# One set of products with ones for a step's two key tiles, after VectorE has added their numerators

## The chip, the cores and the metric

The kernel runs on one core of a Trainium2 chip. A core has a matrix engine (TensorE, in the profile PE, with its weight loads as PEld), three engines for elementwise work (VectorE as DVE, ScalarE as ACT, GpSimd as POOL) and queues that start DMA transfers (SP among them). The engines run side by side, each works through its own instructions in order, and they wait for each other through semaphores. Matrix products land in PSUM, which has eight banks of 512 fp32 columns.

The metric is device time of one execution in microseconds (us), lower is better.

## The reference

One transformer block on `x` of shape (2, 1024, 128), all in fp32: attention, then a mixture of experts. Cut to what matters:

```python
q = (x @ wq).reshape(Bq, Tq, N_KV, N_REP, HEAD_DIM)      # 2 groups of 4 heads
k_lat = (x @ wk_down).reshape(Bq, Tq, N_KV, D_LAT)       # 32 wide
v_lat = (x @ wv_down).reshape(Bq, Tq, N_KV, D_LAT)
k = jnp.einsum('bkhl,ld->bkhd', k_lat, wk_up)
v = jnp.einsum('bkhl,ld->bkhd', v_lat, wv_up)
scores = jnp.einsum('bqhrd,bkhd->bhrqk', q, k) * scale
scores = jnp.where(causal, scores, jnp.finfo(scores.dtype).min)
probs = jax.nn.softmax(scores, axis=-1)
y = jnp.einsum('bhrqk,bkhd->bqhrd', probs, v)
...
x = x + _layernorm(attn(_layernorm(x)))
x = x + _layernorm(moe(_layernorm(x)))    # 32 experts, top 6 of 2 of 4 groups; 16 anchors; shared
```

The softmax divides each query's weighted sum of values by the sum of its numerators over all keys. That sum of numerators is what the change is about.

## The kernel before, in words

**Folding.** The up-projections are folded into the queries and into the output weights, so that keys and values are used 32 wide. Four heads of a group then share TensorE: their 32-row or 32-column strips work side by side.

**Units and steps.** Attention runs over units `(b, g, q)`: batch, group of four heads, block of 256 queries (`QC`). Batch 0 goes through its blocks upwards, batch 1 downwards. A unit has `q + 1` steps `s`, and each step has two key tiles of 128 keys (`pieces`, line 450). A step with `s < q` is full: both tiles count for all 256 queries. The step `s == q` lies on the diagonal: the second tile counts only for the upper 128 queries. There are 40 steps in 16 units, 24 full and 16 on the diagonal.

**What a step does.**
- `numerators` (456): TensorE writes the scores of four heads, keys by queries, into four PSUM banks (464) and adds minus the query's maximum (478). ScalarE takes the exponential into an SBUF tile `pr` (484), 128 keys x 4 heads x up to 512 columns: the first tile's queries, then the second's. On the diagonal GpSimd sets what the mask hides to zero (487). `pr` has three buffers.
- `values` (497): TensorE multiplies `pr` with the values and accumulates in the left half of the bank `o` (501), 32 partitions for a head.
- `sums` (507): TensorE multiplies the same `pr` with a matrix of ones and accumulates in the right half of `o` (510). Each of the 32 rows of a head then holds the sum over the keys.
- After a unit's last step ScalarE copies `o` to SBUF (517) and `normalized` (520) divides: two ScalarE operations, then three of VectorE (530 to 532), put off by `tick`.

**The maxima ahead.** The maxima of later units are found in items (`maxima`, 388): products of queries with keys into four banks `sm` (399), the mask (409), and four or eight reductions on VectorE (416). After a unit's last item, `split` (427) cuts the maxima into three bf16 parts on VectorE, `turn` (436) transposes them on TensorE (443), and VectorE copies the result to `mT` (447), which line 478 reads.

**Order.** The order on TensorE, VectorE, ScalarE and GpSimd is that of the program text. For each step the loop at 575 writes: the scores and numerators of this step, the values of the step before (`weigh`), a transposition if one is ready, a `tick`, one item of maxima, the sums of the step before, another `tick`, and sometimes one more item. A `tick` advances side work by a piece: the normalization, the projections of later tokens (`project`), and from the end of batch 0 on its output projection and routing (`route`, 609: many small VectorE operations, lines 674 to 748).

**PSUM.** Seven banks are handed out in turn under one tag, for the scores, the maxima, the transpositions and all side work. The eighth is `o`.

After attention come the experts (762): 20 chunks for each of four blocks of 512 tokens, three products of 512 columns each, with routing rows that SP loads.

Of the kernel before, what the change touches and what calls it, by code (L numbers as in the profile page):

```python
# [10 lines left out]
F32 = mybir.dt.float32  # L11
BF16 = mybir.dt.bfloat16
AF = mybir.ActivationFunctionType
ALU = mybir.AluOpType
# [3 lines left out]
P = 128  # L18
# [7 lines left out]
def attn_moe_block(  # L26
# [34 lines left out]
    nc = tc.nc  # L61
    B, T, D = x.shape
    NT = T // P
    QC = 256
# [6 lines left out]
    L = wk_up.shape[0]  # L71
    G = wk_down.shape[1] // L
    R = NH // G
    scale = float(P) ** -0.5
    E, _, MI = w_gate.shape
    A, _, AI = anchor_w_gate.shape
# [10 lines left out]
    work = ctx.enter_context(tc.tile_pool(name="work", bufs=2))  # L87
# [3 lines left out]
    def bank(name, dtype=F32):  # L91

        return psum.tile([P, 2048 // mybir.dt.size(dtype)], dtype, tag="s", name=name, bufs=7)

    def acc(name):
        return psum.tile([P, 512], F32, tag="o", name=name, bufs=1)
# [83 lines left out]
    ones32 = const.tile([P, L], F32, name="ones32")  # L180
# [11 lines left out]
    def tables(name):  # L192

        if name != loaded[0]:
            nc.scalar.preload_act_table_set(name)
            loaded[0] = name
# [6 lines left out]
    def tick():  # L203
        for queue in (ends, side):
            while queue:
                if next(queue[0], queue) is not queue:
                    break
                queue.pop(0)
# [30 lines left out]
    def awake(n):  # L239

        idle = bank("idle")
        for _ in range(n):
            nc.tensor.matmul(
                idle, lhsT=ones, rhs=ones.unsqueeze(1).to_broadcast([P, 4, P]),
                start=True, stop=True,
            )
# [189 lines left out]
    def turn(u):  # L436

        b, g, q = u
        parts = neg_parts[units.index(u) % len(neg_parts)]
        pt = bank(f"pm{b}{g}{q}", BF16)  # L440

        for i, j in enumerate((*range(TQ), TQ - 1)):
            nc.tensor.transpose(
                pt[:, ts(i, P)], parts[:, j, :, :].rearrange("p r l -> p (r l)"), ident_bf
            )
        mT = work.tile([P, QC + P], BF16, tag="mT", name=f"mT{b}{g}{q}", bufs=6)
        nc.vector.tensor_copy(mT, pt[:, 0 : QC + P])  # L447
        negT[u] = mT

    def pieces(u, s):  # L450

        if s < u[2]:
            return [(2 * s, 0, 0, QC), (2 * s + 1, QC, 0, QC)]
        return [(2 * s, 0, 0, QC), (2 * s + 1, QC, P, P)]

    def numerators(u, s):

        b, g, q = u
        qT, kT, _ = qkv[b]
        banks = [bank(f"s{b}{g}{q}{s}") for _ in range(R)]  # L460
        for i, (kt, at, lo, n) in enumerate(pieces(u, s)):
            for r in range(R):
                rows = ts(r, L)
                nc.tensor.matmul(  # L464
                    banks[r][:, at : at + n], lhsT=kT[rows, g, ts(kt, P)],
                    rhs=qT[rows, g, q * QC + lo : q * QC + lo + n], start=(i == 0), stop=False,
                    skip_group_check=True,
                )
        mT = negT[u]
        m = at + n  # L470
        for r in range(R):
            rows = ts(r, L)
            if s < q:
                less = mT[rows, 0:QC].unsqueeze(1).to_broadcast([L, 2, QC])
                dst = banks[r].rearrange("p (i c) -> p i c", c=QC)
            else:
                less, dst = mT[rows, :], banks[r][:, 0:m]
            nc.tensor.matmul(  # L478
                dst, lhsT=ones[rows, :], rhs=less, start=False, stop=True, skip_group_check=True
            )  # L480
        tables(EXP_LN)
        pr = work.tile([P, R, 2 * QC], F32, tag="wide", name=f"pr{b}{g}{q}{s}", bufs=3)
        for r in range(R):
            nc.scalar.activation(pr[:, r, 0:m], banks[r][:, 0:m], AF.Exp)  # L484
        if s == q:
            own = pr.rearrange("p r (i c) -> p r i c", c=QC)[:, :, :, 0:P]
            nc.gpsimd.affine_select(  # L487
                out=own, in_=own, compare_op=ALU.is_ge, fill=0.0, base=0,
                pattern=[[0, R], [0, 2], [1, P]], channel_multiplier=-1,
            )  # L490
        return pr
# [5 lines left out]
    def values(u, s, pr, o):  # L497
        b, g, _ = u
        for kt, at, lo, n in pieces(u, s):
            for r in range(R):  # L500
                nc.tensor.matmul(  # L501
                    o[ts(r, L), lo : lo + n], lhsT=qkv[b][2][:, kt, ts(g, L)],
                    rhs=pr[:, r, at : at + n],
                    start=(kt == 0), stop=False, skip_group_check=True,
                )

    def sums(u, s, pr, o):
        for kt, at, lo, n in pieces(u, s):
            for r in range(R):
                nc.tensor.matmul(  # L510
                    o[ts(r, L), QC + lo : QC + lo + n], lhsT=ones32,
                    rhs=pr[:, r, at : at + n], start=False, stop=True, skip_group_check=True,
                )
        b, g, q = u
        if s == q:
            t = work.tile([P, 2 * QC], F32, tag="raw", name=f"raw{b}{g}{q}", bufs=3)
            nc.scalar.copy(t, o)
            ends.append(normalized(u, t))

    def normalized(u, t):  # L520

        b, g, q = u
        own, total = t[:, 0:QC], t[:, QC : 2 * QC]
        r = work.tile([P, QC], F32, tag="rsum", name=f"rsum{b}{g}{q}", bufs=2)
        tables(EXP_LN)
        nc.scalar.activation(r, total, AF.Ln)
        nc.scalar.activation(r, r, AF.Exp, scale=-1.0)
        yield
        ot[u] = work.tile([P, QC], F32, tag="ot", name=f"ot{b}{g}{q}", bufs=NU + 2)
        nc.vector.scalar_tensor_tensor(total, total, -1.0, r, ALU.mult, ALU.mult)  # L530
        nc.vector.tensor_tensor(own, own, r, ALU.mult)
        nc.vector.scalar_tensor_tensor(ot[u], total, 2.0, own, ALU.add, ALU.mult)
        yield

    def attention(done_with):
        items = [(u, gen) for u in units for gen in [maxima(u)] for _ in range(u[2] + 1)]
        through = {u: i + 1 for i, (u, _) in enumerate(items)}


        need = [through[units[0]]]  # L540
        for k in range(1, len(steps)):
            ahead = steps[min(k if k < 4 else k + 1, len(steps) - 1)][0]
            need.append(max(need[-1], through[ahead]))
        done = 0
        turned = 0
        finished = 0

        def one_item():
            nonlocal done, finished
            u, gen = items[done]  # L550
            while projected.get((u[0], u[2] * QC // BC), -1) < u[1]:
                tick()
            assert units.index(u) < turned + len(neg_parts)
            next(gen)
            done += 1
            finished += through[u] == done

        def turn_ready(upto):
            nonlocal turned
            while turned < upto:  # L560
                turn(units[turned])
                turned += 1

        o = {}
        waiting = None

        def weigh(entry):
            u, s, pr = entry
            while projected.get((u[0], u[2] * QC // BC), -1) < G:
                tick()  # L570
            if s == 0:
                o[u] = acc(f"o{u[0]}{u[1]}{u[2]}")
            values(u, s, pr, o[u])

        for k, (u, s) in enumerate(steps):
            while done < need[k]:
                one_item()
                if k == 0:
                    tick()
                    awake(3)  # L580
            ready = finished
            turn_ready(units.index(u) + 1)
            pr = numerators(u, s)
            if waiting:
                weigh(waiting)
            turn_ready(ready)
            tick()


            if done < len(items):  # L590
                one_item()
            if waiting:
                last = waiting[0]
                sums(*waiting, o[last])
                if last[0] != u[0]:
                    done_with(last[0])
            waiting = (u, s, pr)
            tick()
            if any(need[j] - done > j - k - 1 for j in range(k + 1, len(steps))):
                one_item()  # L600
                tick()
        weigh(waiting)
        sums(*waiting, o[waiting[0]])
        done_with(waiting[0][0])


# [282 lines left out]
```

## Time and profile before

Three runs took 479.04, 480.38 and 480.4 us. The profiled execution is one more execution, and all durations below come from it.

| | us |
|---|---|
| median of the runs | 480.38 |
| span of the profiled execution | 478.7 |
| PE busy (share of the span) | 453.1 (95%) |
| DVE busy | 303.3 (63%) |
| ACT busy | 219.6 (46%) |
| POOL busy | 33.5 (7%) |
| products with values, line 501: 640 instructions, busy | 39.4 |
| products with ones, line 510: 640 instructions, busy | 39.3 |
| first score product to last product with ones (attention) | 19.2 to 233.3 |

How to read it: busy time is the time in which an engine had work in flight. It doesn't say who waits for whom; that is in the chain of waits (followed back from the last instruction, at each step to what released it) and in the order of time. An fp32 product is two instructions of TensorE, so that 320 products with ones are 640 instructions. In a row such as `128x512 f32<-128x512 f32 x80 | 58.0, 725 | 2.7` come the shape written and read, the count, the busy time, the mean of one in ns, and the idle time of the engine before them. `x16 ... 1.00` in the chain of waits is a piece of 16 instructions that took 1.00 us.

### The profile page before, as it was taken

The page shows a single profiled execution, that of the slowest core. Times are in us where ns is not written, and L with a number is a line of the kernel's source. Part 1 is how long each engine was busy: PE and PEld are TensorE (multiplying, and loading weights), DVE is VectorE, ACT ScalarE, POOL GpSimd, SP SyncE. Part 2 cuts the span into 40 slices and gives each one's busy share as a digit, 9 for nine tenths or more (in the row PEclk, how much of TensorE's full clock was granted, in tenths as well). Part 3 has the DMA queues.
Part 4 walks back from the last instruction along what each step waited for, and adds up shares of the span by engine and source line. Part 5 has one row for each costly group of instructions (what it writes and reads, how often), then busy time and mean ns, then how long its engine had stood idle before and what let it go on. Part 6 is the DMA issues. An engine that isn't in the chain of part 4 may idle for free.

```text
span 478.7 us, 8959 instructions
## 1 busy us (share of the span) xinstructions
PE 453.1 (95%) x3427; PEld 223.7 (47%) x3427; DVE 303.3 (63%) x943; ACT 219.6 (46%) x427; POOL 33.5 (7%) x55
## 2 busy tenths in 40 slices
PE   8997999999999999988869999999999999999991
PEld 5554554544555555555345444544434444344440
DVE  4468766466756887797335575489656755466552
ACT  3454556554554747746642646432225422252222
POOL 2000000000000201002100110000001100001001
PEclk9999999999999999999979999999999999999996
DMA  7820000000000000000521333223151353124100
GB/s 218 222 86 1 2 1 2 1 1 3 1 1 3 2 1 3 1 2 19 176 68 55 100 109 96 66 83 109 51 163 60 118 134 109 66 91 136 58 1 22
DMA packets 27355, 29.26 MB, mean 61 GB/s; under 512 B 8272, under 2 KB 16112, under 8 KB 27312
## 3 DMA queue, kind: packets, MB, share of 16 engines
q1 hardware_dynamic: 26976, 28.15, 19.5%
q8 instruction: 27, 0.44, 0.4%
q10 hardware_dynamic: 336, 0.54, 0.3%
q14 instruction: 16, 0.13, 0.1%
HBM read 27.23 MB, written 1.44 MB: 60 GB/s over the span
## 4 chain that ended last, share of the span: by engine, by line
PE 70%; DVE 16%; issue 10%; ACT 1%; DMA 1%; POOL 0%; POOLq 0%; ACTq 0%; DVEq 0%
PE pg L775 12%; PE pu L776 12%; PE oacc L785 11%; DVE nm L416 8%; PE sm L399 7%; PE s L464 5%; PE o L501 4%; PE o L510 4%; PE pp L352 3%; PE po L621 2%; DVE parts L432 2%; PE psh L791 2%; DVE nm L434 1%; PE s L478 1%; PE sm L409 1%
## 5 line engine op out<-in xcount | busy, mean ns | idle before, releaser
L416 DVE TENSOR_REDUCE nm<-sm 128x1 f32<-128x512 f32 (+2 forms) x192 | 92.7, 548 | 53.1 <-PE sm L409 37.0
L780 DVE TENSOR_TENSOR hid<-hid,pu 128x512 f32<-128x512 f32 x80 | 54.8, 686 | 75.9 <-PE pu L776 56.8
L484 ACT ACTIVATE pr<-s 128x512 f32<-128x512 f32 (+1 forms) x160 | 75.5, 558 | 55.5 <-PE s L478 55.5
L779 ACT ACTIVATE hid<-pg 128x512 f32<-128x512 f32 x80 | 47.8, 597 | 115.5 <-PE pg L775 103.5
L775 PE MATMUL pg<-hT,wg_sb 128*128 128x512 f32 x160 | 83.4, 603 | 0.0
L776 PE MATMUL pu<-hT,wu_sb 128*128 128x512 f32 x160 | 82.1, 594 | 0.0
L785 PE MATMUL oacc<-hid,wd_sb 128*128 128x512 f32 x160 | 80.9, 595 | 0.0
L781 DVE TENSOR_TENSOR hid<-hid,spread 128x512 f32<-128x512 f32 x80 | 58.0, 725 | 2.7
L776 PEld LDWEIGHTS pu<-hT,wu_sb 128*128 128x128 f32 x160 | 30.7, 192 | 38.8 <-issue 37.9
L785 PEld LDWEIGHTS oacc<-hid,wd_sb 128*128 128x128 f32 x160 | 30.1, 190 | 39.3 <-issue 31.5
L464 PE MATMUL s<-qT,kT 32*128 32x256 f32 (+1 forms) x640 | 46.9, 381 | 1.0 <-DVE nm L416 1.0
L775 PEld LDWEIGHTS pg<-hT,wg_sb 128*128 128x128 f32 x160 | 29.3, 192 | 35.7 <-issue 34.8
L399 PE MATMUL sm<-kT,qT 32*128 32x512 f32 (+3 forms) x384 | 44.3, 525 | 0.8 <-DVE nm L416 0.3
L501 PE MATMUL o<-pr,v 128*32 128x256 f32 (+1 forms) x640 | 39.4, 364 | 2.1 <-POOL pr L487 1.9
L464 PEld LDWEIGHTS s<-qT,kT 32*128 32x128 f32 x640 | 32.0, 184 | 16.2 <-issue 10.1
L510 PE MATMUL o<-pr,ones 128*32 128x256 f32 (+1 forms) x640 | 39.3, 363 | 0.0
L487 POOL TENSOR_SCALAR_AFFINE_SELECT pr<-pr 128x1024 f32<-128x1024 f32 x16 | 17.8, 1112 | 196.3 <-ACT pr L484 196.3
L501 PEld LDWEIGHTS o<-pr,v 128*32 128x32 f32 x640 | 16.7, 109 | 23.2 <-issue 10.1
L510 PEld LDWEIGHTS o<-pr,ones 128*32 128x32 f32 x640 | 17.0, 109 | 20.5 <-issue 11.6
L399 PEld LDWEIGHTS sm<-kT,qT 32*128 32x128 f32 x384 | 16.8, 183 | 11.9 <-issue 4.2
L826 POOL TENSOR_TENSOR y<-y,x 128x512 f32<-128x512 f32 x4 | 5.1, 1267 | 192.3 <-DVE y L295 150.7
L478 PE MATMUL s<-mT,ones 32*128 32x512 bf16 (+1 forms) x160 | 16.9, 353 | 1.5 <-DVE mT L447 1.5
(163 smaller groups left out, 365.1 us busy)
## 6 DMA issues: line engine op xcount, KB each, us to landing
spread<-cw_rows SPq DMA_DIRECT2D x128, 128.0 KB, 2.9
spread<-cw_rows SPq DMA_DIRECT2D x64, 64.0 KB, 2.0
out_dram<-y SPq DMA_DIRECT2D x4, 256.0 KB, 2.3
x<-in_L_attn_x_dram SPq DMA_DIRECT2D x2, 256.0 KB, 4.1
wq_sb<-in_L_attn_wq_dram ACTq DMA_DIRECT2D x2, 256.0 KB, 4.2
wo_sb<-in_L_attn_wo_dram SPq DMA_DIRECT2D x1, 512.0 KB, 6.5
x<-in_L_attn_x_dram SPq DMA_DIRECT2D x1, 512.0 KB, 7.6
cw_rows<-cwT SPq DMA_DIRECT2D x4, 96.0 KB, 1.9
```

The source lines that it names most:

```text
L399: nc.tensor.matmul(banks[r][:, at : at + k1 - k0], lhsT=qT[ts(r, L), g, ts(qt, P)], rhs=kT[ts(r, L), g, k0:k1], start=(at == 0), stop=Fals ...
L416: nc.vector.tensor_reduce(nm[:, k0 // BC, j, r : r + 1], banks[r][:, at : at + k1 - k0], AX.X, ALU.max, negate=True,)
L464: nc.tensor.matmul(banks[r][:, at : at + n], lhsT=kT[rows, g, ts(kt, P)], rhs=qT[rows, g, q * QC + lo : q * QC + lo + n], start=(i == 0), ...
L484: nc.scalar.activation(pr[:, r, 0:m], banks[r][:, 0:m], AF.Exp)
L501: nc.tensor.matmul(o[ts(r, L), lo : lo + n], lhsT=qkv[b][2][:, kt, ts(g, L)], rhs=pr[:, r, at : at + n], start=(kt == 0), stop=False, skip ...
L510: nc.tensor.matmul(o[ts(r, L), QC + lo : QC + lo + n], lhsT=ones32, rhs=pr[:, r, at : at + n], start=False, stop=True, skip_group_check=True,)
L775: nc.tensor.matmul(pg, lhsT=wg_sb[:, c, :], rhs=hT[:, cols], start=True, stop=True)
L776: nc.tensor.matmul(pu, lhsT=wu_sb[:, c, :], rhs=hT[:, cols], start=True, stop=True)
L779: nc.scalar.activation(hid, pg, AF.Silu)
L780: nc.vector.tensor_tensor(hid, hid, pu, ALU.mult)
L781: nc.vector.tensor_tensor(hid, hid, spread, ALU.mult)
L785: nc.tensor.matmul(oacc, lhsT=wd_sb[:, c, :], rhs=hid, start=False, stop=(c == NCH - 1))
```

## The change

`paired` adds, on VectorE, the numerators of a step's two key tiles for all four heads in one instruction, into an SBUF tile `pair` with a single buffer. `sums` multiplies this with ones in place of the two tiles. On a full step that is 1,024 columns added (4 heads x 256) and four products of 256 columns in place of eight. On the diagonal the second tile counts only for the upper 128 queries: these 128 columns a head are added (512 in all), four products of 128 columns take them, and four more take the lower 128 queries from `pr`, in place of four of 256 and four of 128. The addition for a step is written after the scores and numerators of the step that follows, ahead of its `weigh`; for the last step, ahead of the last `weigh`.

```diff
-    def sums(u, s, pr, o):
-        for kt, at, lo, n in pieces(u, s):
+    def paired(u, s, pr):
+
+        pair = work.tile([P, R, QC], F32, tag="pair", name=f"pair{u[0]}{u[1]}{u[2]}{s}", bufs=1)
+        (_, _, _, n0), (_, at, lo, n) = pieces(u, s)
+        nc.vector.tensor_tensor(
+            pair[:, :, lo:n0], pr[:, :, lo:n0], pr[:, :, at : at + n], ALU.add
+        )
+        return [pair[:, :, lo:n0], pr[:, :, 0:lo]] if lo else [pair]
+
+    def sums(u, s, pair, o):
+        hi = QC
+        for part in pair:
+            lo = hi - part.shape[2]
             for r in range(R):
                 nc.tensor.matmul(
-                    o[ts(r, L), QC + lo : QC + lo + n], lhsT=ones32,
-                    rhs=pr[:, r, at : at + n], start=False, stop=True, skip_group_check=True,
+                    o[ts(r, L), QC + lo : QC + hi], lhsT=ones32,
+                    rhs=part[:, r, :], start=False, stop=True, skip_group_check=True,
                 )
+            hi = lo
...
             pr = numerators(u, s)
+            pair = paired(*waiting) if waiting else None
             if waiting:
                 weigh(waiting)
...
-                sums(*waiting, o[last])
+                sums(*waiting[0:2], pair, o[last])
...
+        pair = paired(*waiting)
         weigh(waiting)
-        sums(*waiting, o[waiting[0]])
+        sums(*waiting[0:2], pair, o[waiting[0]])
         done_with(waiting[0][0])
```

## The prediction

> **What bounds the kernel now.** I read the page's head and its chain of waits, then the busy time stretch by stretch, then the order of time.
>
> ```profile
> span 478.7 us, 8959 instructions
> ...
> PE 70%; DVE 16%; issue 10%; ACT 1%; DMA 1%; POOL 0%; POOLq 0%; ACTq 0%; DVEq 0%
> ```
>
> PE's 70% of the chain makes it look like the only bound. The stretches, cut at the first score product of a step (start:end, length, then busy time of PE, PEld, DVE, ACT, POOL), say otherwise:
>
> ```profile
> 42.77:51.80 9.03, 7.79 (x95) 4.33 (x89) 8.69 (x24) 4.30 (x12) 1.10 (x1) 1.00 0.01 2
> ...
> 116.84:134.55 17.71, 17.58 (x255) 8.52 (x251) 11.93 (x27) 9.13 (x19) 1.10 (x1) 1.00 0.01 2
> ...
> 160.15:184.28 24.13, 22.92 (x346) 12.24 (x342) 20.85 (x70) 17.56 (x41) 4.01 (x5) 1.00 0.01 2
> 184.28:195.97 11.69, 11.69 (x159) 7.15 (x155) 5.64 (x15) 7.72 (x16) 1.42 (x5) 1.00 0.00 1
> 195.97:224.92 28.95, 26.03 (x394) 14.85 (x390) 27.36 (x164) 16.76 (x35) 3.51 (x3) 1.00 0.01 2
> ```
>
> At 116.84 (one unit of four steps) PE is full and VectorE has 5.8 us free. At 42.77, 160.15 and 195.97 VectorE is 96%, 86% and 95% busy: there the reductions of the maxima and, from 160, the routing of batch 0 fill it. The order of time in the free stretch shows how near the two engines stand:
>
> ```profile
> 118.92 1.14 PE L399 MATMUL sm<-kT,qT 32*128 32x512 f32 x8
> ...
> 120.00 0.86 PE L510 MATMUL o<-pr,ones 128*32 128x256 f32 x16
> 120.08 2.48 DVE L416 TENSOR_REDUCE nm<-sm 128x1 f32<-128x512 f32 x4 [1.67 <-PE sm L399]
> 120.78 1.17 PE L464 MATMUL s<-qT,kT 32*128 32x256 f32 x16
> ```
>
> Four reductions start 0.09 us after their products end and take 2.48. The next step's scores (L464) take four of seven PSUM banks in turn, and the fourth is the bank of the first reduction. That one took about 0.68 (L416, 128x512), so its bank is free some 0.75 after 120.08, at 120.83, while PE is there at 120.78. Line 416's own view names the wait:
>
> ```profile
> who waited for it (us, times):
>   PEld s L464: 2.3, 4
> ```
>
> So products with ones that become shorter bring L464 forward only until the first reduction is over: 0.84 us after the maxima's products, whatever the sums take.
>
> **What it removes.** 24 of the 40 steps are full (two key tiles for 256 queries), 16 end a unit on the diagonal. Sums in the chain of waits are pieces of 1.00 us (512 columns a head) or, as at 120.06, 0.79 (384): 0.21 for 128 columns. Both kinds become 256 columns: 1.00 - 2 x 0.21 = 0.58. That saves PE 24 x 0.42 + 16 x 0.21 = 13.4 us. Where L464 follows directly, the 0.84 lets through 0.16 of a full step and nothing of a diagonal one; all of it counts only where other products stand between.
>
> **What it adds.** 40 additions on VectorE. No row has 128x1024, so the bounds come from these:
>
> ```profile
> L781 DVE TENSOR_TENSOR hid<-hid,spread 128x512 f32<-128x512 f32 x80 | 58.0, 725 | 2.7
> L780 DVE TENSOR_TENSOR hid<-hid,pu 128x512 f32<-128x512 f32 x80 | 54.8, 686 | 75.9 <-PE pu L776 56.8 <-ACT hid L779 16.0 <-PE pt_h L313 2.3
> ...
> L531 DVE TENSOR_TENSOR raw<-raw,rsum 128x256 f32<-128x256 f32 x16 | 6.7, 418 | 0.0
> ```
>
> 256 more elements cost 0.268 (418 to 686 ns) to 0.307 (to 725). A diagonal addition (4 heads x 128 = 512) is 0.69 to 0.73, a full one (1024) 1.22 to 1.34; I take 0.69 and 1.25, nearest L531 and L780, which run on an undisturbed queue. What follows without a wait starts about 0.09 before the row before it ends (four reductions of 0.68 within 2.48), so in the queue they hold 0.60 and 1.15. All 40 are 24 x 1.15 + 16 x 0.60 = 37 us.
>
> The Trainium skill, "VectorE: DVE Perf Modes", section "The DRAIN you can't avoid", speaks against even that overlap: the next operation is not to start before the pipeline is empty. The overlapping rows above differ from it; by the rule the 17 additions that I find on the path would cost 17 x 0.09 = 1.5 us more.
>
> **What it moves, and the new waits.** An addition stands in VectorE's queue behind the last step's reductions and ahead of the copy of mT, whatever side work comes next, and the next reductions; those in turn hold PE through the banks. It waits for ACT or POOL (the numerators, done over 1 us before the reductions are) and for PE's previous sums, which read the only pair buffer; these end half a us into 2.4 us of reductions. Both cost nothing while reductions stand in front. The products with ones now wait for VectorE. Near 215 and 218 no reductions come, but routing: eight replacements each time, 1.4 us. PE would reach the sums there 1 to 2 us before their addition; but that stretch is VectorE's already, so I count the addition once. The numerators' buffers come free no later. SP's loads of the routing rows are behind routing and shift with it.
>
> **The sum, by stretch.**
> - To 99 us: at 42.77 one full addition, 1.15, with 0.3 idle; at 66 to 75.5 (7.95 of 9.41 busy) a further 0.6 beyond what the idle takes; less 0.42 + 2 x 0.21 of sums that have projections behind them: +0.9.
> - 99 to 160, three units of four steps. Following 116.84 step by step: the second step has reductions 2.40, an addition 1.15 and the unit's normalization 1.1, and its reductions are 0.2 late; the third catches up; at the unit's end split, addition and mT copy make them 0.1 late again. Against that stands 0.16 gained. +0.1 at 1.15 an addition, +0.5 at 1.25 without overlap; I take 0.3 for two units, and 0.7 for the third, where batch 0's statistics stand between split and addition: +1.3.
> - 160.15 to 184.28: 4 x 1.15 + 0.60 = 5.2, with 20.85 makes 26.05 in 24.13: +1.9 if VectorE never idled. It idled 3.3, since it and PE wait for each other in turn; I keep 1.1 of that: +3.0. From 184.28 PE is full and VectorE half idle: -0.4.
> - 195.97 to 224.92: 4 x 1.15 + 2 x 0.60 = 5.8, with 27.36 makes 33.16 in 28.95: +4.2 without idling; it idled 1.6, I keep 1.4: +5.6.
> - To 233: the last steps wait for POOL and ACT, shorter sums bring them 0.3 forward. From there the experts run PE after PE and shift as a whole.
>
> 0.9 + 1.3 + 3.0 - 0.4 + 5.6 - 0.3 = +10.1 on the profiled 478.7, so 488.8. The median of the runs shown, 480.38, is 1.7 above that span; the forecast is 490.5 us.
>
> **Rivals.**
> - *The additions are hidden, PE's saving lands whole* (6%): 480.4 - 13.4 = 467. For it: PE 95% busy, VectorE 63%. Against: the three full stretches and the bank wait. It needs reductions that are nowhere later than now.
> - *The bank wait decides, nothing is late* (7%): 24 x 0.16 = 3.8 at most comes through, less what the full stretches take: 477 to 481. It needs VectorE to take up 5 us per full stretch in idle time that is only 3.3 and 1.6.
> - *PE's new waits lower its clock* (12%): the place is 215 to 225, where sums wait behind routing. In this trace the clock was 0.50 in 246 to 250 and 0.73 in 250 to 254, after PE had waited 3.7 us; 14 products of the output projection took 3.36 in place of 1.98 for 16, the next gate product 1.71 and the next up product 1.17 in place of 0.86: some 2.8 us in all. One or two such dips on top: 493 to 496. It decides once one wait reaches that length; I expect 2 us. The Trainium skill, "TensorE: Matmul & The Clock Gate", part 1, puts the limit at an idle window of about 3.4 us, which the 3.7 here agrees with; by it this rival gives nothing.
> - That sums are not halved is excluded: 24 x 4 + 16 x 8 = 224 logical products in place of 320, two instructions each.
>
> **How the numbers follow.** The forecast has 75%. Its low end has no VectorE idling in the two full stretches (1.9 and 4.2), nothing lost before 160 and -0.7 elsewhere: +5.4, 485.8. Its high end has 1.34 an addition without overlap (17 x 0.19 = 3.2) and all the old idling kept (2.2 + 0.2): +15.7, 496.1. It is widened by 1.9 towards the clock rival and by 1.8 towards the second: 484 to 498. A measurement of this kernel tells 0.3% (1.4 us) from no change. Faster by more: 6% and half the second rival, 9%. Same: 4%. Slower: 87%.
>
> **What would show it.** Right: 448 instructions of products with ones, about 39.3 - 13.4 = 26 us busy in place of 39.3; 40 additions of 1.2 and 0.7 us; VectorE over 95% busy in the stretches that were 160 to 184 and 196 to 225; waits of PE for the pair near 215; the scores starting 0.84 after the maxima's products. Wrong: reductions that start as early as now, an addition well over 1.34, or an attention stage that ends before 233 us.

## The result, and the profile after

The changed kernel takes 486.85 us (median of four runs, 485.83 to 487.63), the kernel before 480.39 beside it (479.04 to 481.04): a ratio of 1.0148, with a 95% interval from 1.0121 to 1.0175. The ratios are estimated from the single executions and differ a little from the quotients of the medians, here 1.0134. The profiled execution spans 485.57 us, 6.83 more than that of before (478.74). From the page, the span, the engines' shares of the chain of waits, and two groups of instructions:

```profile
span 485.6 us, 8657 instructions
...
PE 65%; DVE 19%; issue 12%; ACT 1%; POOL 1%; DMA 1%; POOLq 0%; ACTq 0%; DVEq 0%
...
L511 DVE TENSOR_TENSOR pair<-pr 128x1024 f32<-128x1024 f32 (+1 forms) x40 | 41.5, 1037 | 3.7 <-POOL pr L487 3.7
...
L521 PE MATMUL o<-pair,ones 128*32 128x256 f32 (+1 forms) x320 | 22.1, 348 | 5.9 <-DVE pair L511 5.9
```

40 additions keep VectorE busy for 41.5 us. The products with ones are 448 instructions (these 320 and 128 more that read `pr`), in all 25.6 us busy in place of 39.3: the 22.1 of the row and the 6.4 of the others overlap. PE's share of the chain fell from 70% to 65%, VectorE's rose from 16% to 19%. The same stretches as before (start:end, length, busy time of PE, PEld, DVE, ACT, POOL, then the granted clock, DMA share and GB/s), cut at the same steps. The granted clock is TensorE's, 1.00 being full speed; at 118.57 begins the unit of four steps that began at 116.84 before:

```profile
42.35:54.48 12.13, 9.19 (x87) 5.27 (x82) 11.52 (x29) 4.30 (x12) 1.10 (x1) 0.84 0.01 1
...
118.57:136.04 17.47, 16.92 (x231) 8.38 (x227) 15.72 (x31) 9.13 (x19) 1.84 (x2) 1.00 0.01 2
162.19:187.17 24.98, 22.28 (x314) 11.84 (x310) 24.33 (x74) 17.33 (x41) 5.05 (x5) 1.00 0.01 2
187.17:199.07 11.90, 11.74 (x151) 7.13 (x148) 8.17 (x19) 8.18 (x17) 1.43 (x5) 1.00 0.01 2
199.07:232.96 33.89, 28.19 (x361) 15.34 (x357) 32.71 (x171) 16.74 (x35) 2.99 (x3) 0.90 0.00 1
```

Against the rows of before: the first is 3.10 us longer, and its clock is 0.84. The unit of four steps, where VectorE has room, is 0.24 shorter. The last is 4.94 longer, with VectorE busy for 97% of it. The stretch at 162.19 grew by only 0.85, although VectorE is 97% busy there too. What TensorE waits for (us in total, number of waits, longest):

```profile
PE o L521 <- DVE pair L511: 5.9, 5, 2.1
PE pm L443 <- DVE parts L432: 5.8, 10, 1.1
PE s L464 <- DVE nm L416: 4.9, 7, 1.4
```

The first row is new; the other two were 3.4 and 1.0 us before. The longest wait of the first, in the order of time (start, length, what, and in brackets the idle time of the engine before it):

```profile
222.71 0.18 DVE L739 MATCH_REPLACE8 erep<-etop,ms 128x40 f32<-128x40 f32 x1
222.81 1.21 DVE L511 TENSOR_TENSOR pair<-pr 128x1024 f32<-128x1024 f32 x1
223.94 0.35 DVE L447 COPY mT<-pm 128x384 bf16<-128x384 bf16 x1
224.08 0.64 PE L521 MATMUL o<-pair,ones 128*32 128x256 f32 x8 [2.12 <-DVE pair L511]
224.65 2.06 PE L464 MATMUL s<-qT,kT 32*128 32x256 f32 x16
```

The addition is queued behind eight replacements of the routing (the first row is the last of them). It takes 1.21 us, as long as an undisturbed one, and TensorE stands still for 2.12. The score products behind it take 2.06 us, where undisturbed ones take 1.17: the clock was halved from 224.73 to 228.14.

### The profile page after: what moved, and what is told of

It is laid out like the page before. It is cut to its first block, busy times and chain, and to the rows that moved or that the text cites. A ratio compares the mean times of both kernels' runs of the same rounds, so it can differ in the third digit from the quotient of the medians.

```text
span 485.6 us, 8657 instructions
## 1 busy us (share of the span) xinstructions
PE 449.7 (93%) x3235; PEld 221.1 (46%) x3235; DVE 339.2 (70%) x983; ACT 219.7 (45%) x427; POOL 36.7 (8%) x55
## 4 chain that ended last, share of the span: by engine, by line
PE 65%; DVE 19%; issue 12%; ACT 1%; POOL 1%; DMA 1%; POOLq 0%; ACTq 0%; DVEq 0%
PE pg L789 12%; PE pu L790 12%; PE oacc L799 11%; DVE nm L416 9%; PE sm L399 6%; PE s L464 5%; PE o L501 4%; PE pp L352 3%; DVE pair L511 3%; PE o L521 2%; PE po L635 2%; DVE parts L432 2%; PE psh L805 2%; PE s L478 1%; PE sm L409 1%
## 5 line engine op out<-in xcount | busy, mean ns | idle before, releaser
L484 ACT ACTIVATE pr<-s 128x512 f32<-128x512 f32 (+1 forms) x160 | 75.5, 558 | 62.8 <-PE s L478 61.8
L464 PE MATMUL s<-qT,kT 32*128 32x256 f32 (+1 forms) x640 | 53.8, 396 | 4.9 <-DVE nm L416 4.9
L399 PE MATMUL sm<-kT,qT 32*128 32x512 f32 (+3 forms) x384 | 46.4, 547 | 0.8 <-DVE nm L416 0.5
L464 PEld LDWEIGHTS s<-qT,kT 32*128 32x128 f32 x640 | 35.9, 190 | 22.4 <-issue 10.0
L511 DVE TENSOR_TENSOR pair<-pr 128x1024 f32<-128x1024 f32 (+1 forms) x40 | 41.5, 1037 | 3.7 <-POOL pr L487 3.7
L501 PE MATMUL o<-pr,v 128*32 128x256 f32 (+1 forms) x640 | 41.4, 378 | 2.1 <-POOL pr L487 2.1
L487 POOL TENSOR_SCALAR_AFFINE_SELECT pr<-pr 128x1024 f32<-128x1024 f32 x16 | 21.0, 1315 | 199.6 <-ACT pr L484 173.7
L521 PE MATMUL o<-pair,ones 128*32 128x256 f32 (+1 forms) x320 | 22.1, 348 | 5.9 <-DVE pair L511 5.9
L399 PEld LDWEIGHTS sm<-kT,qT 32*128 32x128 f32 x384 | 17.9, 195 | 12.5 <-issue 4.6
L478 PE MATMUL s<-mT,ones 32*128 32x512 bf16 (+1 forms) x160 | 21.3, 371 | 1.5 <-DVE mT L447 1.5
```

The costliest lines, as they stand in the source:

```text
L399: nc.tensor.matmul(banks[r][:, at : at + k1 - k0], lhsT=qT[ts(r, L), g, ts(qt, P)], rhs=kT[ts(r, L), g, k0:k1], start=(at == 0), stop=Fals ...
L464: nc.tensor.matmul(banks[r][:, at : at + n], lhsT=kT[rows, g, ts(kt, P)], rhs=qT[rows, g, q * QC + lo : q * QC + lo + n], start=(i == 0), ...
L501: nc.tensor.matmul(o[ts(r, L), lo : lo + n], lhsT=qkv[b][2][:, kt, ts(g, L)], rhs=pr[:, r, at : at + n], start=(kt == 0), stop=False, skip ...
L511: nc.vector.tensor_tensor(pair[:, :, lo:n0], pr[:, :, lo:n0], pr[:, :, at : at + n], ALU.add)
```

## The experiments

### The additions alone, the shorter products alone, and GpSimd in place of VectorE

```diff
  e1_add_only: the additions stay, the sums read pr as before
-    def sums(u, s, pair, o):            +    def sums(u, s, pr, o):
-                    rhs=part[:, r, :],  +                    rhs=pr[:, r, at : at + n],
  e2_no_add: no addition, the first key tile stands for both
-        return [pair[:, :, lo:n0], pr[:, :, 0:lo]] if lo else [pair]
+        return [pr[:, :, lo:n0], pr[:, :, 0:lo]] if lo else [pr[:, :, 0:n0]]
  e3_gpsimd
-        nc.vector.tensor_tensor(
+        nc.gpsimd.tensor_tensor(
```

> The 40 additions stay on VectorE, but nothing reads them: the products with ones read the numerators as before, so TensorE saves nothing and never waits for an addition. Theory (an addition costs where VectorE's queue is already full, and the shorter products bring little, since the next scores wait for the bank of the first reduction): nearly all of the loss is here, +5 to +10 over before, 485 to 490. Rival (TensorE's saving of 13.4 lands whole in the changed kernel, whose 6.5 of loss is then 20 of additions and waits): about 480.4 + 20 = 500, or clearly over 493.

> No addition: the halved products with ones read the first key tile's numerators alone, the second tile is left out of the sums (so the outputs are not the reference's). TensorE saves the same 13.4 us of products, VectorE gets nothing more. Theory (the bank of the first reduction holds the next scores 0.84 us after the maxima's products): 0.16 of each full step outside the stretches that VectorE fills, and the whole 0.42 only where other products stand between, 3 to 6 us in all: 474 to 477.5. Rival (the saving lands whole): 467.

> The same additions on GpSimd, which is 7% busy. From its rows (128x256 0.82 us, 128x512 1.27) a full addition should take about 2.2 us and end before the products with ones reach it, over 3 us after the numerators. Theory (VectorE's queue is what costs): most of the loss goes, 474 to 480. Rival (it is TensorE's waits for an addition, or the port that the two engines seem to share: an addition took 2.12 us in place of 1.21 while GpSimd's masking ran): 484 or more.

The kernel before took 479.95 beside them.

- e1: 492.54 us, ratio 1.0276 (1.0246 to 1.0306). The additions cost 12.6 us when nothing is saved. That misses the theory's range by 2.5 and stops half a us short of the rival's 493, so e1 alone doesn't decide between the two.
- e2: 475.21 us, ratio 0.9905 (0.9888 to 0.9922); nine of its ten runs lie between 473.72 and 476.35, one at 481.69. Of the 13.4 us of products that go, 4.7 arrive in the end. The theory's range holds, and the rival in which the saving lands whole falls. Together, 12.6 lost and 4.7 gained make 7.9; the change itself lost 6.5.
- e3: 533.55 us, ratio 1.1135 (1.1095 to 1.1176). The theory failed, and the rival's waits of TensorE for an addition are what the trace shows.

In the unit that begins at 100.13 in e1, the length is 17.70 us, as long as before to 0.01, although VectorE is busy for 15.72 of it in place of 11.91, and the unit behind it is the same. So there the additions cost nothing by themselves. From the first score product to the last step e1 loses 12.6: 6.47 in its last stretch (195.97 to 224.92 before), which takes 35.42 us, 2.5 up to 99 us, 1.7 between 160.15 and 195.97, 0.6 behind the last stretch, and 1.4 in a single step (156.21 to 160.15 before), which takes 5.31 us in place of 3.94, with VectorE busy for 5.17 of it. In e1 TensorE never waits for an addition; the 6.47 are therefore VectorE's time and not such waits.

What e3's additions meet, in the order of time at the end of one unit:

```profile
129.40 1.10 POOL L487 TENSOR_SCALAR_AFFINE_SELECT pr<-pr 128x1024 f32<-128x1024 f32 x1 [4.40 <-ACT pr L484]
...
130.47 2.34 POOL L511 TENSOR_TENSOR pair<-pr 128x1024 f32<-128x1024 f32 x1
...
132.86 0.64 PE L521 MATMUL o<-pair,ones 128*32 128x256 f32 x8 [2.28 <-POOL pair L511]
```

A full addition takes GpSimd 2.34 us, nearly twice VectorE's 1.21, and where the next step lies on the diagonal it queues behind that step's mask, which is GpSimd's as well. The sums waited 36.0 us in 14 waits, and the mean clock was 0.919.

### What keeps the rest of TensorE's saving

The prediction said that the bank of the first reduction holds the next scores. To test that, the reductions of the maxima were shortened, once with the products of before and once with those of e2.

```diff
-  nm[:, k0 // BC, j, r : r + 1], banks[r][:, at : at + k1 - k0], AX.X,
+  nm[:, k0 // BC, j, r : r + 1], banks[r][:, at : at + (k1 - k0) // 2], AX.X,
```

> The kernel before, its reductions of the maxima taking the first half of each piece of a bank only (the other half of the keys is left out of the maxima). It is the base for the next kernel: reductions of some 0.4 in place of 0.68 us, so the banks come free early and VectorE is full nowhere. The theory of the bank wait and its rival expect the same of this one: 465 to 478, less than before by what the two full stretches and the waits for maxima give up.

> The halved products of e2 (first key tile alone in the sums, no addition) together with the halved reductions. Theory (of the 13.4 us that TensorE saves, e2 showed 4.7, because the first bank is held by its reduction until 0.84 us after the maxima's products): with that bank free earlier the saving lands nearly whole, 10 to 13.4 us under the kernel with halved reductions alone. Rival (the saving is kept by something else, such as ScalarE's exponentials or the step's own order): 4 to 6.5 us under it.

h1 took 468.87 us, ratio 0.9786 (0.9759 to 0.9813), h2 462.02, ratio 0.9645 (0.9617 to 0.9674). h1's maxima bound only half of the exponents, so it measures what the reductions cost and is no version of the kernel. With long reductions the shorter products bring 4.7 us, with short ones 6.85. By the medians the theory's 10 to 13.4 is missed, and so is its rival's range, from above. The traces say where. From the first score product to the start of the first step of the last stretch (195.97 before) e2 is 3.9 us shorter than the kernel before (172.9 against 176.8), but h2 is 8.95 shorter than h1 (161.63 against 170.58), of some 10.7 (20 full steps by 0.42 and 11 on the diagonal by 0.21). A unit of four steps falls by 1.5 from h1 to h2 (17.49 to 15.98), the whole of 3 x 0.42 + 0.21; from before to e2 only by 0.53. So up to there the long reductions are what held the saving. Shorter ones also empty VectorE's queue, so the unit of four steps, where VectorE had room before, is the clean case for the bank wait. In the last stretch h2 is a microsecond longer than h1 (28.17 against 27.17): TensorE meets the routing earlier and waits for it 2.59 us in one place, where h1 waits 1.50, and the clock is halved from 204.35 on.

The hold itself, in e2 and then in h2, the same step:

```profile
116.84 1.14 PE L399 MATMUL sm<-kT,qT 32*128 32x512 f32 x8
...
118.00 2.48 DVE L416 TENSOR_REDUCE nm<-sm 128x1 f32<-128x512 f32 x4 [1.48 <-PE sm L399]
118.49 1.17 PE L464 MATMUL s<-qT,kT 32*128 32x256 f32 x15
...
119.50 0.37 PE L464 MATMUL s<-qT,kT 32*128 32x256 f32 x1
...
120.02 1.07 PE L501 MATMUL o<-pr,v 128*32 128x256 f32 x16
```

```profile
107.61 1.14 PE L399 MATMUL sm<-kT,qT 32*128 32x512 f32 x8
...
108.77 1.42 DVE L416 TENSOR_REDUCE nm<-sm 128x1 f32<-128x256 f32 x4 [2.30 <-PE sm L399]
109.25 1.15 PE L464 MATMUL s<-qT,kT 32*128 32x256 f32 x16
...
110.54 1.07 PE L501 MATMUL o<-pr,v 128*32 128x256 f32 x16
```

In e2 the scores start 0.51 us after the maxima's products end (117.98), earlier than in the kernel before (0.72), but one of the sixteen comes late, and the products with values start 2.04 after that end. In the kernel before they do so too: 122.10 after 120.06. In h2 it is 1.79 after 108.75. The lateness begins with the fourth score product, the first to write the bank of the first reduction. In e2's trace three start at 118.49 to 118.50 and the fourth at 118.75, when that reduction has ended (118.69); in h2 all four start within 0.02. The changed kernel has the same delay in this step, 122.54 and 122.80. The products came forward and what follows did not, until the reductions were shorter.

### Where the additions cost

```diff
+        if steps.index((u, s)) not in ADDED:
+            return [(pr[:, :, at : at + n], lo, n) for _, at, lo, n in pieces(u, s)]
  f1_room_only: ADDED = (4, 6, 8, 9, 12, 13, 14, 16, 17, 18, 20, 21, 30)
  f2_not_first: ADDED = range(4, 40)
  f3_not_full:  ADDED = (*range(25), 38, 39)
```

> Additions and halved products in 13 of the 40 steps, those in which VectorE has idle time to take them (counted from 0: 4, 6, 8, 9, 12, 13, 14, 16, 17, 18, 20, 21, 30); the other 27 sum every key tile as the kernel before does. Theory (the additions cost only where VectorE is full; elsewhere the shorter products come through by 0.2 to 0.4 us a step): of the gains that the comparison of the steps shows, 0.43 at three steps, 0.22 to 0.24 at each of the others that gain, about 2.5 us in all, so 477.5 to 479, and no new wait of PE over 1 us. Rival (each addition delays the maxima behind it, wherever it stands): 13 x 0.3 us and more lost, 482 or above.

> The change without its first four steps: steps 0 to 3 sum every key tile as the kernel before does, steps 4 to 39 as changed. Theory (the additions of the first stretch cost 3.7 us there, by VectorE's full queue and two halvings of the clock, and nothing later makes up for them): 482.5 to 484, with no halving of the clock before 60 us. Rival (the lateness of the first stretch is taken up later, or only moves to the next stretch in which VectorE is full): 485.5 to 487.5.

> The change without steps 25 to 37, the two stretches in which the routing of batch 0 fills VectorE as well: there every key tile is summed as the kernel before does. Theory (these stretches cost 0.9 and 5.0 us by their own additions): 480.5 to 482. Rival (what is lost there was carried in from earlier steps, or the clock's halvings cost it): 484 or above.

The kernel before took 479.42 beside them.

- f3: 480.30 us, ratio 1.0016 (0.9993 to 1.0039), 0.2 under the theory's range. Without the additions of steps 25 to 37 the loss can't be told from nothing; the last stretch is 28.78 us long. The rival falls.
- f2: 485.63 us (483.08 to 486.91), ratio 1.0115 (1.0075 to 1.0155). The theory's range is missed, and the median lies at the lower end of the rival's. In the trace the stretch of steps 2 and 3 takes 17.18 in place of 21.03 us, and no later stretch takes that up or adds to it (24.98 and 33.92 us in the two that VectorE fills, as in the changed kernel). But one halving of the clock stayed there, behind a wait for `mT` that the kernel before has as well, and one came to it at 237.70, behind the waits that end the attention stage.
- f1: 478.72 us (476.22 to 482.27), ratio 0.9989 (0.9964 to 1.0015). Inside the theory's range, but it can't be told from the kernel before: its own twelve runs lie 6 us apart. The trace has a new wait of TensorE of 1.10 us (at 76.05), where the theory wanted none over 1.

### The clock

Runs of one kernel differ, and the clock is one reason. Here are two executions with the same wait of 3.69 us ahead of the last output projection, each cut at the times at which its clock can change: the kernel before, then f1.

```profile
241.91:245.32 3.41, 0.98 (x4) 0.38 (x2) 1.30 (x3) 2.02 (x3) 0.00 (x0) 1.00 0.25 77
245.32:252.15 6.83, 5.57 (x17) 4.17 (x18) 1.17 (x4) 1.05 (x2) 0.00 (x0) 0.50 0.15 41
```

```profile
239.84:243.26 3.42, 1.51 (x5) 0.60 (x4) 1.02 (x3) 2.51 (x4) 0.00 (x0) 1.00 0.23 87
243.26:246.67 3.41, 1.63 (x14) 1.63 (x15) 1.69 (x4) 0.00 (x0) 0.00 (x0) 1.00 0.25 74
```

In the kernel before most of the wait falls into one window of 3.41 us, TensorE is busy for 0.29 of it, and the next 6.83 us run at half clock. In f1 two windows share the wait (0.44 and 0.48 busy), and the clock stays: the fourteen products behind it take 1.83 us in place of 3.36. Every change of the clock within these traces falls on such a grid of 3.41 us, at an offset that differs from one execution to the next. Two kernels fill TensorE's waits to take this out.

```diff
  f4_awake, on the changed kernel: busy(n, ...) issues n products of zeros
+                if i == 0 and r == 2 and steps.index((u, s)) == 33:
+                    busy(4, banks[0][:, 0:n], zeros32[ts(0, L), :], qT[ts(0, L), g, 0:n])
+        if steps.index((u, s)) == 2:
+            busy(4, banks[0][:, 0:QC], zeros32[ts(0, L), :], qT[ts(0, L), g, 0:QC])
...
+        for _ in range({2: 3, 34: 4}.get(steps.index((u, s)), 0)):
+            busy(1, o[ts(0, L), 0:QC], zeros32[:, 0:L], pr[:, 0, 0:QC])
  the last output projection's wait, in g1, g2 and g3
+            if b == 1 and c == 0:
+                for _ in range(14):
+                    nc.tensor.matmul(
+                        po, lhsT=ones, rhs=ones.unsqueeze(1).to_broadcast([P, 4, P]),
+                        start=True, stop=True,
+                    )
```

> The change as it is, with 15 products of zeros on TensorE (11 or 12 of them in place of its longest waits of 1.4 to 2.1 us in the attention stage: ahead of the maxima's subtraction in step 2, among the scores of step 33, ahead of the sums of steps 2 and 34); they add zeros to banks that are open. Theory of the clock (part of the loss is the halved clock that follows windows of 3.41 us in which TensorE is busy for less than 0.58 of the time; five such halvings lie in the attention stage of the changed kernel, none in that of the kernel before): three to five of them vanish, each giving back 0.5 to 1.4 us: 482.5 to 485.5. Rival (VectorE sets the pace there and the clock costs nothing): the time stays at 486 to 488 though the halvings go. If they don't go, the window's share is not what decides.

f4 took 485.95 us, ratio 1.0139 (1.0111 to 1.0167): its theory missed, the rival's number is nearly met. All halvings of the attention stage went; behind the last output projection two windows are halved. The trace splits the question by place. Steps 2 and 3 take 17.92 in place of 21.03 us, so there the clock did cost 3.1. The last stretch is as long as with two halvings (33.89):

```profile
195.83:229.70 33.87, 28.60 (x378) 16.16 (x374) 32.73 (x170) 16.86 (x35) 3.16 (x3) 1.00 0.01 2
```

So there the halvings cost nothing: VectorE, busy for 32.73 of 33.87 us, sets the pace.

> The kernel before with two fillings of TensorE and no other change: 4 products of zeros ahead of the maxima's subtraction in step 2 (a wait of 1.46 us) and 14 products of ones into the bank of the last output projection, ahead of it (a wait of 3.7 us; the projection overwrites them). Theory of the window (the clock is halved for the 3.41 us after a window of 3.41 us in which TensorE was busy for less than some 0.55; behind the 3.7 us wait each halved window costs 1.3 to 1.6 us, and it takes none, one or two by where the wait falls on the windows): 476.5 to 478, with a smaller spread than the 477.2 to 480.9 of the kernel before. Rival (the halving follows from the wait itself, or its cost is hidden by later work): 479 to 480.5.

> The changed kernel with the waits of steps 2, 33 and 34 filled as in f4, and that of the last output projection as well. Against the kernel before with its own two waits filled, what is left is the change without the clock: by the steps of f4's trace, 214.4 in place of 208.2 us from the first score product to the last step, so about 6 us apart: 482.5 to 484.5. If the difference of the two is still 6.5 to 8 us, the clock had no part in the loss; if it is under 5, it had a larger part than the steps of one trace show.

> Additions and halved products in 13 steps chosen anew from the step tables (4, 5, 8, 9, 10, 12, 13, 14, 16, 17, 18, 20, 30), every key tile summed as before in the others, with the same two fillings as the kernel before has in g2. Theory (the steps' gains add up: 0.40 at 4 and 5, 0.65 from 8 to 10, 0.47 from 12 to 18, 0.17 at 20, 0.21 at 30, 1.9 us in all): 1.5 to 2.3 us under g2, so 474.5 to 476.5. Rival (what a step gains the next one waits for, as step 8 did in f1): within 0.7 us of g2.

g2 is the kernel before with 4 and 14 products in its two waits, g3 is f4 with the 14 as well, and g1 is a choice of 13 steps, those that had gained in the traces so far, with both of g2's fillings (`ADDED = (4, 5, 8, 9, 10, 12, 13, 14, 16, 17, 18, 20, 30)`). The kernel before took 478.96 beside them.

| | us | runs | against the kernel before |
|---|---|---|---|
| g2, before, waits filled | 476.19 | 476.03 to 476.21 | 0.9940 (0.9928 to 0.9953) |
| g3, changed, waits filled | 484.31 | 482.84 to 484.67 | 1.0104 (1.0086 to 1.0123) |
| g1, 13 steps, waits filled | 474.53 | 474.45 to 474.71 | 0.9907 (0.9891 to 0.9923) |

No window is halved in the three traces before their last 8 us; every trace ends at half clock. g2's runs lie within 0.2 us, where those of the kernel before spread over 2 us (g3's still spread over 1.8); filling two waits brings 2.8 us. Of g2, TensorE around the wait that was 3.69:

```profile
240.95 3.19 PE L629 MATMUL po<-ones 128*128 128x512 bf16 x14
...
245.03 1.83 PE L635 MATMUL po<-ao,ot 128*128 128x128 f32 x14 [0.67 <-DVE ot L540]
```

g3 stands 8.12 us above g2, more than the 6 expected. Of the two traces' 8.1 us, 1.77 lie ahead of the first score product (17.71 and 19.48), where nothing of the change has run; in the traces with full reductions that product falls either at 17.5 to 17.8 or, as in the kernel before, at 18.9 to 19.5, and why was not tried. That share of the difference therefore can't be put down to the change. From there to the first product of the last step it is 208.12 and 214.42: the change costs 6.30 us with the clock out of the way. The stretches of g2, then of g3:

```profile
41.28:50.31 9.03, 7.79 (x95) 4.33 (x89) 8.69 (x24) 4.31 (x12) 1.10 (x1) 1.00 0.00 0
...
158.62:182.75 24.13, 22.92 (x347) 12.25 (x343) 20.85 (x70) 17.56 (x41) 4.01 (x5) 1.00 0.01 2
...
194.44:223.37 28.93, 26.03 (x394) 14.83 (x390) 27.34 (x164) 16.76 (x35) 3.51 (x3) 1.00 0.01 2
```

```profile
42.78:53.36 10.58, 9.05 (x94) 4.69 (x89) 10.24 (x25) 4.30 (x12) 1.10 (x1) 1.00 0.00 0
...
160.90:185.87 24.97, 22.27 (x314) 11.84 (x311) 24.32 (x74) 17.34 (x41) 5.05 (x5) 1.00 0.01 2
...
197.76:231.65 33.89, 28.61 (x378) 16.16 (x374) 32.74 (x170) 16.86 (x35) 3.16 (x3) 1.00 0.01 2
```

g1 stands 1.66 us under g2, as expected from adding up single steps: that much the change brings in steps chosen because VectorE has room in them. It is the fastest version here that computes the maxima in full, but 2.8 of its 4.4 us are the filled waits and have nothing to do with the change.

## Why the prediction was right, and where it was not

The forecast of 490.5 us lies 3.6 above the result, its range holds it, and the mechanism is the predicted one: the additions fill an engine that is already the bound in some stretches (f3, e1), and the bank wait keeps much of what TensorE saves (e2, h2). Term by term, against g2 and g3, whose clock is undisturbed, and against the two profiled executions:

| | predicted | g2 to g3 | before to after |
|---|---|---|---|
| to 99 us | +0.9 | +0.41 | +3.65 |
| 99 to 160 | +1.3 | +0.10 | +0.09 |
| 160.15 to 184.28 | +3.0 | +0.84 | +0.85 |
| 184.28 to 195.97 | -0.4 | +0.20 | +0.21 |
| 195.97 to 224.92 | +5.6 | +4.96 | +4.94 |
| what is left to the last step | -0.3 | -0.21 | -0.20 |
| sum | +10.1 | +6.30 | +9.54 |

The span of after grew by 6.83 and not by 9.54 because its first score product came 1.70 us earlier (17.49 for 19.19), and what follows the last step's first product took 1.01 less, with one halved window behind the last output projection in place of two.

- *195.97 to 224.92* holds four fifths of the 6.30. "it idled 1.6, I keep 1.4": VectorE is busy for 32.71 of 33.89, so 1.2 stayed, and 33.16 of work was right to 0.5.
- *160.15 to 184.28* is the step that failed most: "4 x 1.15 + 0.60 = 5.2, with 20.85 makes 26.05". VectorE's busy time grew by 3.5, to 24.33, and 0.65 of idling stayed in place of 1.1. Four instructions were gained for five additions: a reduction of 0.68 now lies behind the stretch's end, where VectorE is half idle. Four subtractions of `split` took 0.69 in all in place of 1.23. What else shortened the sum was not resolved. The prediction took all work of a stretch as due by its end, and work that runs late can be done in the next one.
- *99 to 160*: the three units were to lose 1.3 and lost 0.1. The addition alone costs nothing in the first two (e1) and the shorter products alone gain 0.53 a unit (e2); together they gained 0.22 and 0.24 in these two and lost 0.55 in the third, where the prediction had put its largest share, 0.7. The step-by-step lateness of 0.1 to 0.5 was too dear.
- *To 99 us*: the clock-free loss is half of the term, the traced one four times it. By f4, 3.1 of the 3.65 are the clock. Inside the term two sizes were wrong: from g2 to g3 the step at 42.77 lost 1.55 (9.03 to 10.58) and not 1.15, its addition being held up by GpSimd's mask (last section), and 66 to 75.5 gained 0.40 (9.40 to 9.00) where a further 0.6 was to be lost.
- *The bank*: the saving that it lets through was put at "24 x 0.16 = 3.8 at most"; e2 measured 4.7. "0.84 us after the maxima's products" is not when the scores start (0.51), but nearly when the fourth of them does (0.77). The reductions start 0.02 after those products end (120.08 after 118.92 + 1.14) and not "0.09", which makes up the difference. The hold passes on to the start of the products with values.
- *Additions*: 1.21 and 0.68 undisturbed, for 1.25 and 0.69. The mean of the full ones is 1.275, because three of them took 1.47 to 2.12, the longest beside GpSimd's mask. The overlap of 0.09 is there: the copy behind the addition at 222.81 starts at 223.94, 0.08 before 222.81 + 1.21.
- *The single buffer for the pair*, put at nothing, agrees: the only idle time of VectorE before an addition is 3.7 us for the mask, ahead of the last two. A second buffer was not tried.
- *Products with ones*: 25.6 us busy, for 26.
- *The waits near 215 and 218*: the first became 2.12 us, for "1 to 2". Behind it TensorE ran at half clock and met no second wait; in f4, at full clock, that one was 1.42.

The rival of the clock was mis-stated. "It decides once one wait reaches that length", 3.7 us, is wrong: halvings followed waits of 1.4 to 2.1 us. What goes with them is the share of a window in which TensorE is busy, and not the length of one wait (last section). But the loss doesn't need the clock: without any halving it is 6.30. By the medians, filling the waits brings 2.8 us before and 2.5 after (486.85 to 484.31, measured at different times; 2.1 by the two ratios), and g3's later first score product (19.48 for 17.49 in the traces) hides part of the second. Counted from that product to the end, the traces give 2.76 before (459.55 to 456.79) and 4.98 after (468.08 to 463.10). So in the profiled executions the clock adds 2.2 us to the loss; how much it adds in the others was not measured. The free-running window of some 3.4 us in the Trainium skill, "TensorE: Matmul & The Clock Gate", Part 1, agrees with the grid of 3.41 us. Its rule that no idle gap over some 3.4 us should stand (Part 1, "HAM oscillation") is too mild for this trace, where 2.12 us inside one window sufficed.

So the trace's +9.54 beside the predicted +10.1 is luck: two terms too large by 3.4 together, and a clock in the first stretch, 3.1, that was not in the sum. The measured 6.5 beside the clock-free 6.30 is no better proof, since in the traces it is 9.54 less 1.70 and 1.01.

## What to carry to other kernels

Moving work from the engine with the largest busy time to one with room pays only in the stretches in which that room exists: here 13 of 40 steps, chosen with the traces at hand, gain 1.7 us, and all 40 lose 6.3. A saving on TensorE arrives as far as the next bank is free, so shorten what holds the bank before shortening the products. And a microsecond or two of TensorE's waiting can cost as much again through the clock where TensorE sets the pace (3.1 us in steps 2 and 3), and nothing where VectorE does (33.87 and 33.89 us). Filling the waits also narrowed the runs of g1 and g2 to 0.3 us, enough to tell 0.35% apart.

## What the runs showed of the hardware

**The clock.** Between 26 and 262 us of all 14 traces, each of the 24 windows at full clock in which TensorE was busy for less than 0.44 of 3.41 us was followed by a halved one. Of 30 between 0.44 and 0.60 eight were, of 871 above 0.60 two. The bounds were chosen afterwards, to part the cases. TensorE's busy time is modelled, so the share may not be what the clock counts, and what decides in between stays open: the same wait of 1.46 us in step 2 (0.57 busy) halved the clock in six traces and left it in the kernel before and in e2.

**VectorE and GpSimd.** In the changed kernel an addition that starts just after the mask takes 0.9 us longer:

```profile
47.13 1.10 POOL L487 TENSOR_SCALAR_AFFINE_SELECT pr<-pr 128x1024 f32<-128x1024 f32 x1 [17.09 <-ACT pr L484]
47.19 2.12 DVE L511 TENSOR_TENSOR pair<-pr 128x1024 f32<-128x1024 f32 x1
...
49.36 0.64 PE L521 MATMUL o<-pair,ones 128*32 128x256 f32 x8 [1.53 <-DVE pair L511]
```

2.12 is about 1.10 less 0.06 and another 1.1, as if the addition had run when the mask was done. At 176.30, where both start together, the addition took 1.19 and the mask 2.14 in place of 1.10. The Trainium skill, "SBUF — State Buffer", section "SBUF: two separate sides", has the rule, which agrees: a VectorE operation with two SBUF inputs and a GpSimd operation that reads SBUF lock each other out for a whole instruction. The prediction left this out. The wait of 1.53 us that follows lies in the window whose low share, 0.55, preceded the first stretch's longer halving, 50.65 to 57.48.
